# Layer 0's weight product on 64-row halves of the TensorE array, and the first hop tile by tile

## The chip, the cores and the metric

The kernel runs on one core of a Trainium2 chip. The metric is the device time of one execution in microseconds (us); lower is better. Times quoted as "median" are over several executions; the profile is of one execution, whose own time is given beside its span (the time from its first to its last instruction).

## The reference, cut to what matters

Two graph layers on x of shape (8, 2048, 64), with one adjacency matrix of 2048 x 2048, all in fp32. Each layer needs the features x, one hop A x and a second hop 2 A (A x) - x; it multiplies the three by weights, adds a bias and the input, and normalises each row of 64.

```python
# layer 0: the weights differ from node to node, through an embedding of D = 16
w   = einsum('nd,dkio->nkio', embedding, weight)      # K = 3 terms
b   = einsum('nd,do->no', embedding, bias)
x_g = stack of x, A x, 2 A (A x) - x
x   = layernorm(x + einsum('bnki,nkio->bno', x_g, w) + b)
# layer 1: one weight for all nodes; both supports are the same A, so five terms fold to three
x_cat = concat(x, Ax, 2AAx - x, Ax, 2AAx - x)
x   = layernorm(x + x_cat @ weight + bias)
```

## The kernel before, in words

The 2048 nodes are cut into 16 tiles `t` of 128 partitions. `z[t]` is a resident SBUF tile that holds for each of the 8 batches the 64 features of x (slot 0) and the 64 of A x (slot 1), interleaved: its shape is [128, 8, 2, 64]. A block of the adjacency is 128 columns of output by all 2048 rows, 1 MB, cut by `k` into 16 squares of 128 x 128.

`hop(t, s, ks)` (L122 to L129) sums 16 fp32 matmuls over `k` into one PSUM bank: stationary operand the square `blocks[t][:, k, :]`, moving operand the 512 columns of `z[k]`, slot `s`. The profile counts every fp32 matmul as two MATMUL records and two LDWEIGHTS records.

Each layer has two passes over the tiles. The first pass forms A x and copies it by ScalarE into slot 1 (L245). The second pass (L254 to L265) forms A A x; VectorE makes `x2` from it (L259). The weight product of a tile runs one tile behind: `transposes` (L131 to L144) turns `z[t]` and `x2` on TensorE, 12 transposes of 128 x 128 a tile, and ScalarE copies the results to SBUF as `t01` (for each batch 64 rows of x above 64 rows of A x) and `t2` (64 rows of an even batch above 64 of the odd one). Then `mix0` or `mix1` follows.

`mix0` (L180 to L199, layer 0) loops over 4 pairs of batches and 2 halves of D: 8 groups a tile. A group fills a PSUM tile `pm` of two banks, bank `j` for batch `j` of the pair: L189 does two matmuls with a contraction of 128 rows (x and A x together, against `w01`), L192 two with 64 rows (the second hop, against `w2`), the even batch on rows 0 to 63, the odd one on rows 64 to 127. VectorE then folds the group with 8 instructions (L196), one for each d, each multiplying 128 columns of `pm` by a column of the embedding and adding them to slot 0 of `z[t]` in place. The pool `ps_mix` holds two such groups. `layernorm` (L146 to L178) ends the tile with VectorE, GpSimd and ScalarE.

`mix1` (L201 to L219, layer 1) sums 12 matmuls a tile into one bank: 4 of 128 columns against `v2` (two copies of the weight on the diagonal) and 8 of 64 columns against `v01`.

[...]The first 8 blocks stay for the whole run in `low` (8 MB); the other 8 go through a pool of `SLOTS = 4` buffers, loaded again in every pass by `load_high` on SP's queue.

The start: 16 transfers of x on ScalarE's queue (L53, 256 KB each, in rows of 256 B because `z` is interleaved) and 16 on SP's queue (L54), each with square `k` of all 8 low blocks (512 KB in rows of 512 B). `first_sums` (L224 to L237) uses them as they come: for each `k`, 8 matmuls, one into each of the 8 PSUM banks (two of each of the three pools). The second half of the first hop, the 8 high tiles, follows tile by tile. The parameters (embedding, `w01`, `w2`, bias, `v01`, `v2`) come on GpSimd's queue.

The order of instructions on each engine is set by the tile scheduler at build time. On TensorE the order around the change is: `first_sums` with the bias matmuls (L96, L119) between them, eight hops, then for each tile transposes, hop and `mix0`.

Of the kernel before, what the change touches and what calls it, by code (L numbers as in the profile page):

```python
# [8 lines left out]
F32 = mybir.dt.float32  # L9
AF = mybir.ActivationFunctionType  # L10
ALU = mybir.AluOpType
# [3 lines left out]
P = 128  # L15
B, N, C = 8, 2048, 64
NT = N // P
D = 16
EPS = 1e-5
LOW = 8  # L20
SLOTS = 4
# [3 lines left out]
def gnn_kernel(  # L25
# [22 lines left out]
    z = [zpool.tile([P, B, 2, C], F32, tag=f"z{t}", name=f"z{t}") for t in range(NT)]  # L48


    low = zpool.tile([P, LOW, NT, P], F32, tag="low", name="low")
    for k in range(NT):
        nc.scalar.dma_start(out=z[k][:, :, 0, :], in_=x[k])  # L53
        nc.sync.dma_start(out=low[:, :, k, :], in_=adj[0:LOW, :, k, :].rearrange("t m n -> m t n"))  # L54
    apool = ctx.enter_context(tc.tile_pool(name="adj", bufs=SLOTS))
    blocks = {t: low[:, t] for t in range(LOW)}

    def load_block(t, tag):
        a = apool.tile([P, NT, P], F32, tag="a", name=f"a{t}_{tag}")
        nc.sync.dma_start(out=a, in_=adj[t])  # L60
        blocks[t] = a

    high = list(range(LOW, NT))

    def load_high(i, tag):
        if i < NT - LOW:
            load_block(high[i], tag)

    for i in range(SLOTS):
        load_high(i, 0)  # L70
# [6 lines left out]
    w01 = const.tile([P, D, C], F32, tag="w01", name="w01")  # L77
    w2 = const.tile([P, D, C], F32, tag="w2", name="w2")
    v01 = const.tile([P, C], F32, tag="v01", name="v01")
    v2 = const.tile([P, P], F32, tag="v2", name="v2")  # L80
    bias1 = const.tile([P, C], F32, tag="bias1", name="bias1")

    nc.gpsimd.dma_start(out=emb_sb, in_=emb.rearrange("(t p) d -> p t d", p=P))
    for k in range(2):
        nc.gpsimd.dma_start(out=w01[k * C : (k + 1) * C], in_=w0[:, k].rearrange("d i o -> i d o"))
    for h in range(2):
        nc.gpsimd.dma_start(out=w2[h * C : (h + 1) * C], in_=w0[:, 2].rearrange("d i o -> i d o"))
# [3 lines left out]
    for g in range(2):  # L91
        eT = work.tile([D, N // 2], F32, tag="t01", name=f"eT{g}")
        nc.gpsimd.dma_start(out=eT, in_=embT[:, g * (N // 2) : (g + 1) * (N // 2)])
        pb = ps_tp.tile([P, 8, C], F32, tag="tp", name=f"pb{g}")
        for j in range(8):
            nc.tensor.matmul(pb[:, j, :], lhsT=eT[:, j * P : (j + 1) * P], rhs=b0_sb, start=True, stop=True)  # L96
        nc.vector.tensor_copy(ebias[:, g * 8 : (g + 1) * 8, :], pb)


    v01b = work.tile([P, C], F32, tag="x2", name="v01b")  # L100
    nc.vector.memset(v01b, 0.0)
    nc.gpsimd.dma_start(out=v01, in_=w1[0 : 2 * C, :])
    nc.gpsimd.dma_start(out=v01b[C:P, :], in_=w1[3 * C : 4 * C, :])
    nc.vector.tensor_add(v01, v01, v01b)
    v2b = work.tile([P, P], F32, tag="t2", name="v2b")
    nc.vector.memset(v2, 0.0)
    nc.vector.memset(v2b, 0.0)
    for h in range(2):
        q = slice(h * C, (h + 1) * C)
        nc.gpsimd.dma_start(out=v2[q, q], in_=w1[2 * C : 3 * C, :])  # L110
        nc.gpsimd.dma_start(out=v2b[q, q], in_=w1[4 * C : 5 * C, :])
    nc.vector.tensor_add(v2, v2, v2b)
# [8 lines left out]

    def hop(t, s, ks):  # L122

        ph = ps_hop.tile([P, B, C], F32, tag="hop", name="ph")
        for j, k in enumerate(ks):
            nc.tensor.matmul(  # L126
                ph, lhsT=blocks[t][:, k, :], rhs=z[k][:, :, s, :], start=(j == 0), stop=(j == NT - 1)
            )
        return ph  # L129

    def transposes(t, x2):  # L131

        t01 = work.tile([P, B, P], F32, tag="t01", name="t01")
        t2 = work.tile([P, B // 2, P], F32, tag="t2", name="t2")
        for g in range(2):
            pt = ps_tp.tile([P, 4, P], F32, tag="tp", name="pt")
            for j in range(4):
                nc.tensor.transpose(pt[:, j, :], z[t][:, g * 4 + j, :, :], ident)  # L138
            nc.scalar.copy(t01[:, g * 4 : (g + 1) * 4, :], pt)  # L139
        pt = ps_tp.tile([P, 4, P], F32, tag="tp", name="pt")  # L140
        for j in range(4):
            nc.tensor.transpose(pt[:, j, :], x2[:, 2 * j : 2 * j + 2, :], ident)  # L142
        nc.scalar.copy(t2, pt)
        return t01, t2  # L144
# [35 lines left out]
    def mix0(t, t01, t2):  # L180

        acc = z[t][:, :, 0, :]
        nc.gpsimd.tensor_tensor(acc, acc, ebias[:, t : t + 1, :].to_broadcast([P, B, C]), ALU.add)  # L183
        for bp in range(B // 2):
            for dh in range(2):
                pm = ps_mix.tile([P, 2, D // 2, C], F32, tag="mix", name="pm")
                ds = slice(dh * (D // 2), (dh + 1) * (D // 2))
                for j in range(2):
                    nc.tensor.matmul(pm[:, j], lhsT=t01[:, 2 * bp + j, :], rhs=w01[:, ds, :], start=True, stop=False)  # L189
                for j in range(2):  # L190
                    q = slice(j * C, (j + 1) * C)
                    nc.tensor.matmul(pm[:, j], lhsT=t2[q, bp, :], rhs=w2[q, ds, :], start=False, stop=True)  # L192
                part = acc[:, 2 * bp : 2 * bp + 2, :]
                for d in range(D // 2):
                    dd = dh * (D // 2) + d
                    nc.vector.scalar_tensor_tensor(  # L196
                        part, pm[:, :, d, :], emb_sb[:, t, dd : dd + 1], part, ALU.mult, ALU.add
                    )
        layernorm(acc, acc)  # L199

    def mix1(t, t01, t2):  # L201

        pm = ps_mix.tile([P, B, C], F32, tag="mix", name="pm1")
        for bp in range(B // 2):
            nc.tensor.matmul(  # L205
                pm[:, 2 * bp : 2 * bp + 2, :], lhsT=t2[:, bp, :], rhs=v2, start=(bp == 0), stop=False,
                skip_group_check=True,
            )
            for j in range(2):
                b = 2 * bp + j  # L210
                nc.tensor.matmul(  # L211
                    pm[:, b, :], lhsT=t01[:, b, :], rhs=v01, start=False, stop=(b == B - 1), skip_group_check=True
                )
        acc = work.tile([P, B, C], F32, tag="acc", name="acc")
        nc.gpsimd.tensor_tensor(acc, z[t][:, :, 0, :], bias1.unsqueeze(1).to_broadcast([P, B, C]), ALU.add)
        nc.vector.tensor_tensor(acc, pm, acc, ALU.add)
        y = work.tile([P, B, C], F32, tag="y", name="y")
        layernorm(y, acc)
        nc.gpsimd.dma_start(out=out[t], in_=y)  # L219

    ks = list(range(NT))
    order = list(range(LOW)) + high

    def first_sums():  # L224

        accs = [ps_hop.tile([P, B, C], F32, tag="hop", name="ph") for _ in range(2)]
        accs += [ps_tp.tile([P, B, C], F32, tag="tp", name="pt") for _ in range(2)]
        for _ in range(2):
            pm = ps_mix.tile([P, 2, B, C], F32, tag="mix", name="pm")
            accs += [pm[:, 0], pm[:, 1]]  # L230
        for k in ks:
            for t in range(LOW):
                nc.tensor.matmul(  # L233
                    accs[t], lhsT=low[:, t, k, :], rhs=z[k][:, :, 0, :], start=(k == 0), stop=(k == NT - 1)
                )
        for t in range(LOW):
            nc.scalar.copy(z[t][:, :, 1, :], accs[t])  # L237

    for layer, mix in enumerate((mix0, mix1)):

        if layer == 0:
            first_sums()
        for t in order[LOW:] if layer == 0 else order:
            ph = hop(t, 0, ks)
            nc.scalar.copy(z[t][:, :, 1, :], ph)  # L245
            if t in high:
                load_high(high.index(t) + SLOTS, 2 * layer)
        ks = order


        behind = None
        for i in range(SLOTS):
            load_high(i, 2 * layer + 1)
        for t in order:  # L254
            if behind is not None:
                tr = transposes(*behind)
            ph = hop(t, 1, ks)
            x2 = work.tile([P, B, C], F32, tag="x2", name="x2")
            nc.vector.scalar_tensor_tensor(x2, ph, 2.0, z[t][:, :, 0, :], ALU.mult, ALU.subtract)  # L259
            if t in high:  # L260
                load_high(high.index(t) + SLOTS, 2 * layer + 1)
            if behind is not None:
                mix(behind[0], *tr)
            behind = (t, x2)
        mix(behind[0], *transposes(*behind))  # L265
        for i in range(SLOTS):
            if layer == 0:
                load_high(i, 2)
# [29 lines left out]
```

## Time and profile before

| | us |
|---|---|
| median of 3 executions (lowest, highest) | 1397.78 (1396.38, 1402.31) |
| the profiled execution's own time | 1397.78 |
| its span | 1395.2 |
| from the start to the end of `first_sums` | 129.0 |
| second half of the first hop, 8 tiles | 129.0 to 238.7 |
| layer 0's second pass with `mix0`, 16 tiles at 40.0 each, the last without a hop of its own | 238.7 to 880.8 |
| layer 1's first pass, 16 hops | 880.8 to 1100.5 |
| layer 1's second pass with `mix1`, 16 tiles at 17.68 each | 1100.5 to 1375.2 |
| the last tile's product and normalisation, and the last store | 1375.2 to 1395.2 |

The 2.6 us between the profiled execution's time and its span lie before the first and after the last instruction. The stages are read from the timeline: a stage ends where TensorE begins the next one's matmuls. The granted TensorE clock is 0.996 of full speed over the span.

### The profile page before, as it was taken

What the parts mean: (1) busy time and instruction counts of PE and PEld (TensorE: products, weight loads), DVE (VectorE), ACT (ScalarE), POOL (GpSimd) and SP (SyncE); (2) the same over time, 40 slices, a digit from 0 to 9 for tenths busy, and PEclk for the clock granted to TensorE, in tenths of its full rate; (3) what the DMA queues carried; (4) which work ended last, traced back from release to release, by engine and by line L of the source; (5) the groups of instructions that cost most, each with busy time, mean ns of one, the idle gap of its engine ahead of it and who ended that gap; (6) DMA issues with size and microseconds to landing.
All of it is one profiled execution on the core that took longest, in us unless ns stands there. A gap on an engine that the chain in (4) does not pass through costs nothing.

```text
span 1395.2 us, 10043 instructions
## 1 busy us (share of the span) xinstructions
PE 1357.0 (97%) x3874; PEld 601.4 (43%) x3874; DVE 476.2 (34%) x1369; ACT 99.5 (7%) x194; POOL 126.9 (9%) x133
## 2 busy tenths in 40 slices
PE   7999999999999999999999999999999999999996
PEld 3444444433333333333333333444444455555553
DVE  0000000266766666667666668300000012222222
ACT  0001000010000000000000000000000001111111
POOL 2000000011000000000000000000000012222222
PEclk9999999999999999999999999999999999999998
DMA  9900212000000000000000000000012100012100
GB/s 227 296 0 0 91 61 90 0 1 0 0 1 0 0 1 31 31 1 30 31 31 30 31 31 1 0 0 0 31 67 84 61 8 16 16 46 70 51 16 23
DMA packets 39903, 52.40 MB, mean 38 GB/s; under 512 B 17936, under 2 KB 34400, under 8 KB 35760
## 3 DMA queue, kind: packets, MB, share of 16 engines
q1 hardware_dynamic: 21248, 41.95, 9.4%
q10 hardware_dynamic: 16640, 4.20, 1.7%
q0 software_dynamic: 1968, 5.63, 1.3%
q8 instruction: 30, 0.49, 0.1%
q14 instruction: 17, 0.14, 0.0%
HBM read 47.57 MB, written 4.19 MB: 37 GB/s over the span
## 4 chain that ended last, share of the span: by engine, by line
PE 92%; DVE 4%; issue 1%; DMA 1%; POOL 0%; ACT 0%; ACTq 0%; POOLq 0%; DVEq 0%
PE ph L126 55%; PE pm L189 15%; PE pm L192 8%; DVE z L196 4%; PE pm L233 4%; PE pt L138 2%; PE ph L233 2%; PE pt L233 2%; PE pm L211 2%; PE pm L205 1%; DMA z<-in_x 1%; PE pt L142 1%; PE pb L96 0%; POOL xc L160 0%; DVE ln_s L156 0%
## 5 line engine op out<-in xcount | busy, mean ns | idle before, releaser
L126 PE MATMUL ph<-z,a 128*128 128x512 f32 x1024 | 445.1, 592 | 0.0
L196 DVE SCALAR_TENSOR_TENSOR z<-pm,emb_sb,z 128x128 f32<-128x128 f32 x1024 | 359.0, 351 | 74.0 <-PE pm L192 33.6
L126 PE MATMUL ph<-z,low 128*128 128x512 f32 x768 | 335.3, 592 | 0.0
L126 PEld LDWEIGHTS ph<-z,a 128*128 128x128 f32 x1024 | 192.1, 190 | 229.6 <-issue 229.6
L189 PE MATMUL pm<-w,t 128*128 128x512 f32 x512 | 249.5, 609 | 15.7 <-DVE z L196 6.3
L259 DVE SCALAR_TENSOR_TENSOR x<-ph,z 128x512 f32<-128x512 f32 x32 | 22.1, 692 | 687.7 <-PE ph L126 687.7
L126 PEld LDWEIGHTS ph<-z,low 128*128 128x128 f32 x768 | 143.5, 190 | 170.4 <-issue 170.4
L189 PEld LDWEIGHTS pm<-w,t 128*128 128x128 f32 x512 | 88.0, 189 | 172.9 <-PE pm L192 91.0
L192 PE MATMUL pm<-w,t 64*128 64x512 f32 x512 | 144.5, 641 | 0.0
L139 ACT COPY t<-pt 128x512 f32<-128x512 f32 x64 | 34.4, 589 | 736.9 <-PE pt L138 736.9
L183 POOL TENSOR_TENSOR z<-z,ebias 128x512 f32<-128x512 f32 x16 | 20.4, 1275 | 714.5 <-PE pt L138 714.5
L192 PEld LDWEIGHTS pm<-w,t 64*128 64x128 f32 x512 | 38.5, 184 | 97.1 <-issue 97.1
L233 PE MATMUL pm<-z,low 128*128 128x512 f32 x128 | 58.6, 600 | 0.0
L160 POOL TENSOR_TENSOR xc<-acc,ln_nm 128x512 f32<-128x512 f32 x16 | 16.5, 1033 | 409.7 <-DVE ln_nm L158 405.3
L233 PE MATMUL ph<-z,low 128*128 128x512 f32 x64 | 33.8, 653 | 9.8 <-DMA z<-in_x 9.8
L164 DVE TENSOR_REDUCE ln_ss<-sq 128x8 f32<-128x512 f32 x32 | 21.9, 686 | 60.4 <-ACT sq L162 60.4
L233 PEld LDWEIGHTS pm<-z,low 128*128 128x128 f32 x128 | 25.0, 196 | 31.7 <-issue 31.6
L245 ACT COPY z<-ph 128x512 f32<-128x512 f32 x24 | 14.1, 586 | 307.0 <-PE ph L126 307.0
L211 PE MATMUL pm<-v,t 128*128 128x64 f32 x256 | 35.6, 262 | 0.0
L138 PE MATMUL pt<-ident,z 128*128 128x128 f32 x256 | 34.1, 276 | 0.0
L138 PEld LDWEIGHTS pt<-ident,z 128*128 128x128 f32 x256 | 28.4, 144 | 12.4 <-issue 12.4
L211 PEld LDWEIGHTS pm<-v,t 128*128 128x128 f32 x256 | 33.7, 192 | 0.0
(58 smaller groups left out, 363.1 us busy)
## 6 DMA issues: line engine op xcount, KB each, us to landing
a<-in_adj SPq DMA_DIRECT2D x32, 1024.0 KB, 4.8
low<-in_adj SPq DMA_DIRECT2D x16, 512.0 KB, 12.5
z<-in_x ACTq DMA_DIRECT2D x16, 256.0 KB, 12.9
out<-y POOLq DMA_DIRECT2D x16, 256.0 KB, 2.3
w<-in_w POOLq DMA_DIRECT2D x4, 256.0 KB, 10.1
emb_sb<-in_emb POOLq DMA_DIRECT2D x1, 128.0 KB, 9.3
eT<-in_embT POOLq DMA_DIRECT2D x2, 64.0 KB, 10.8
v<-in_w POOLq DMA_DIRECT2D x1, 32.0 KB, 8.0
```

Source lines behind the costliest of these rows:

```text
L126: nc.tensor.matmul(ph, lhsT=blocks[t][:, k, :], rhs=z[k][:, :, s, :], start=(j == 0), stop=(j == NT - 1))
L138: nc.tensor.transpose(pt[:, j, :], z[t][:, g * 4 + j, :, :], ident)
L139: nc.scalar.copy(t01[:, g * 4 : (g + 1) * 4, :], pt)
L160: nc.gpsimd.tensor_tensor(xc, src, wide(nm), ALU.add)
L164: nc.vector.tensor_reduce(ss, sq, AX.X, ALU.add)
L183: nc.gpsimd.tensor_tensor(acc, acc, ebias[:, t : t + 1, :].to_broadcast([P, B, C]), ALU.add)
L189: nc.tensor.matmul(pm[:, j], lhsT=t01[:, 2 * bp + j, :], rhs=w01[:, ds, :], start=True, stop=False)
L192: nc.tensor.matmul(pm[:, j], lhsT=t2[q, bp, :], rhs=w2[q, ds, :], start=False, stop=True)
L196: nc.vector.scalar_tensor_tensor(part, pm[:, :, d, :], emb_sb[:, t, dd : dd + 1], part, ALU.mult, ALU.add)
L211: nc.tensor.matmul(pm[:, b, :], lhsT=t01[:, b, :], rhs=v01, start=False, stop=(b == B - 1), skip_group_check=True)
L233: nc.tensor.matmul(accs[t], lhsT=low[:, t, k, :], rhs=z[k][:, :, 0, :], start=(k == 0), stop=(k == NT - 1))
L259: nc.vector.scalar_tensor_tensor(x2, ph, 2.0, z[t][:, :, 0, :], ALU.mult, ALU.subtract)
```

## The change

Layer 0's product is done wholly with a contraction of 64 rows. `z[t]` is now [128, 2, 8, 64], so that slot 0 and slot 1 are each 512 contiguous columns; a transpose of 128 columns takes one slot of two neighbouring batches, and all three terms come out as `t2` did: even batch above, odd batch below. A group of `mix0` is then 6 matmuls of 64 rows, alternating between the lower and the upper rows, against weights that are held twice, in both halves of the partitions (`w[0]`, `w[1]`, `w[2]`). `mix1` becomes 12 matmuls of 128 columns against block-diagonal weights `v[0]` to `v[2]`.

`first_sums` and `low` are gone. All 16 blocks go through one pool of 11 buffers; each pass begins with the 11 blocks that are still resident from the pass before (`next_order`), and loads 5. The first pass is 16 plain hops. SP's queue begins with 11 transfers of 1 MB in rows of 8 KB; x comes on ScalarE's queue as before, now in rows of 2 KB. GpSimd's queue brings six transfers of 256 KB for layer 0's weights in place of four. On TensorE the built order now begins with tile 0's 16 matmuls, `k` from 0 to 15, then tile 1's, among which the bias matmuls come.

```diff
-LOW = 8
-SLOTS = 4
+SLOTS = 11
...
-    z = [zpool.tile([P, B, 2, C], F32, tag=f"z{t}", name=f"z{t}") for t in range(NT)]
-    low = zpool.tile([P, LOW, NT, P], F32, tag="low", name="low")
-    for k in range(NT):
-        nc.scalar.dma_start(out=z[k][:, :, 0, :], in_=x[k])
-        nc.sync.dma_start(out=low[:, :, k, :], in_=adj[0:LOW, :, k, :].rearrange("t m n -> m t n"))
...
+    z = [zpool.tile([P, 2, B, C], F32, tag=f"z{t}", name=f"z{t}") for t in range(NT)]
...
+    for t in range(NT):
+        nc.scalar.dma_start(out=z[t][:, 0], in_=x[t])
...
+    for k in range(3):
+        for h in range(2):
+            nc.gpsimd.dma_start(out=w[k][h * C : (h + 1) * C], in_=w0[:, k].rearrange("d i o -> i d o"))
...
+    order = list(range(NT))
+    for i in range(SLOTS):
+        load_block(order[i], 0)
+
+    def next_order(o):
+        return o[NT - SLOTS :] + o[: NT - SLOTS]
...
+    def prefetch(o, i, tag):
+        if i + SLOTS < NT:
+            load_block(o[i + SLOTS], tag)
...
     def transposes(t, x2):
+        out = []
+        for s in range(3):
+            tt = work.tile([P, B // 2, P], F32, tag=f"t{s}", name=f"t{s}")
+            pt = ps_tp.tile([P, B // 2, P], F32, tag="tp", name="pt")
+            for j in range(B // 2):
+                pair = x2[:, 2 * j : 2 * j + 2, :] if s == 2 else z[t][:, s, 2 * j : 2 * j + 2]
+                nc.tensor.transpose(pt[:, j, :], pair, ident)
+            nc.scalar.copy(tt, pt)
+            out.append(tt)
+        return out
...
     (mix0)
-                for j in range(2):
-                    nc.tensor.matmul(pm[:, j], lhsT=t01[:, 2 * bp + j, :], rhs=w01[:, ds, :], start=True, stop=False)
-                for j in range(2):
-                    q = slice(j * C, (j + 1) * C)
-                    nc.tensor.matmul(pm[:, j], lhsT=t2[q, bp, :], rhs=w2[q, ds, :], start=False, stop=True)
+                for k in range(3):
+                    for j in range(2):
+                        q = slice(j * C, (j + 1) * C)
+                        nc.tensor.matmul(
+                            pm[:, j], lhsT=tt[k][q, bp, :], rhs=w[k][q, ds, :], start=(k == 0), stop=(k == 2)
+                        )
...
     (mix1)
+            for k in range(3):
                 nc.tensor.matmul(
+                    pm[:, 2 * bp : 2 * bp + 2, :], lhsT=tt[k][:, bp, :], rhs=v[k],
+                    start=(bp == 0 and k == 0), stop=(bp == B // 2 - 1 and k == 2), skip_group_check=True,
                 )
...
-    def first_sums():
-        accs = [ps_hop.tile([P, B, C], F32, tag="hop", name="ph") for _ in range(2)]
-        accs += [ps_tp.tile([P, B, C], F32, tag="tp", name="pt") for _ in range(2)]
-        for _ in range(2):
-            pm = ps_mix.tile([P, 2, B, C], F32, tag="mix", name="pm")
-            accs += [pm[:, 0], pm[:, 1]]
-        for k in ks:
-            for t in range(LOW):
-                nc.tensor.matmul(
-                    accs[t], lhsT=low[:, t, k, :], rhs=z[k][:, :, 0, :], start=(k == 0), stop=(k == NT - 1)
-                )
-        for t in range(LOW):
-            nc.scalar.copy(z[t][:, :, 1, :], accs[t])
...
+        for i, t in enumerate(order):
             ph = hop(t, 0, ks)
+            nc.scalar.copy(z[t][:, 1], ph)
+            prefetch(order, i, 2 * layer)
         ks = order
+        order = next_order(order)
```

## The prediction

> **What bounds the kernel now.** I read the page first, then the timeline of one tile of layer 0, then the start and its transfers.
>
> ```profile
> PE 1357.0 (97%) x3874; PEld 601.4 (43%) x3874; DVE 476.2 (34%) x1369; ACT 99.5 (7%) x194; POOL 126.9 (9%) x133
> L196 DVE SCALAR_TENSOR_TENSOR z<-pm,emb_sb,z 128x128 f32<-128x128 f32 x1024 | 359.0, 351 | 74.0 <-PE pm L192 33.6
> L189 PE MATMUL pm<-w,t 128*128 128x512 f32 x512 | 249.5, 609 | 15.7 <-DVE z L196 6.3
> ```
>
> TensorE looks like the bound everywhere, at 97%. That is an average. Only L189 shows it waiting for VectorE, and that is the stage that the change rewrites. The timeline of one tile there (start, length, both in us):
>
> ```profile
> 267.50 1.88 PE L189 MATMUL pm<-w,t 128*128 128x512 f32 x4
> 269.31 1.13 PE L192 MATMUL pm<-w,t 64*128 64x512 f32 x4
> 270.37 1.98 PE L189 MATMUL pm<-w,t 128*128 128x512 f32 x4
> 270.60 21.84 DVE L196 SCALAR_TENSOR_TENSOR z<-pm,emb_sb,z 128x128 f32<-128x128 f32 x56 [2.21 <-PE pm L192]
> 272.29 1.13 PE L192 MATMUL pm<-w,t 64*128 64x512 f32 x4
> 273.80 1.96 PE L189 MATMUL pm<-w,t 128*128 128x512 f32 x4 [0.39 <-DVE z L196]
> 276.96 1.95 PE L189 MATMUL pm<-w,t 128*128 128x512 f32 x4
> ...
> 289.54 1.96 PE L189 MATMUL pm<-w,t 128*128 128x512 f32 x4 [0.19 <-DVE z L196]
> 291.42 1.13 PE L192 MATMUL pm<-w,t 64*128 64x512 f32 x4
> 292.48 1.09 PE L138 MATMUL pt<-ident,z 128*128 128x128 f32 x8
> ```
>
> VectorE folds 56 slices in 21.84 us, 0.390 each from start to start, so a group of 8 takes it 3.12. From 273.80 to 289.54 TensorE begins a group every 3.15 (15.74 / 5): VectorE's pace. TensorE itself needs less: the second group's L189 begins at 270.37, 2.87 after the first, and a group that follows another takes 289.54 to 292.48 = 2.94. Inside it one record costs 0.43 (a hop of 32 takes 13.73). L192's four records take only 1.06 (269.31 to 270.37), two slots of 0.43 and 0.2 more: lower and upper half do run side by side. So the product is bound by VectorE by 0.2 us a group, and by TensorE only at its two ends.
>
> The start is bound by transfers. The first two lines give issue length in ns (least/median/most) and the first and last issue in us; the next two give count, KB each and median us to landing; the last two are windows whose final figure is GB/s.
>
> ```profile
> L53 ACTq DMA_DIRECT2D z<-in_x x16: 635/2926/6362, 0.7 to 49.5; - x16
> L54 SPq DMA_DIRECT2D low<-in_adj x16: 424/2837/7294, 0.7 to 47.9; - x16
> low<-in_adj SPq DMA_DIRECT2D x16, 512.0 KB, 12.5
> z<-in_x ACTq DMA_DIRECT2D x16, 256.0 KB, 12.9
> 48.00:50.00 2.00, 2.00 (x6) 0.87 (x5) 0.00 (x0) 0.00 (x0) 0.00 (x0) 1.00 1.26 261
> 62.00:64.00 2.00, 2.00 (x6) 0.86 (x5) 0.00 (x0) 0.00 (x0) 0.00 (x0) 1.00 1.05 435
> ```
>
> The two queues advance together, although each transfer of x carries half the bytes of one of `low`. What is equal is the number of rows (1024 of 256 B against 1024 of 512 B). So the engines share by packets, not by bytes. TensorE nevertheless keeps busy from 17.5 on, because each x tile that lands feeds eight sums.
>
> **What the Trainium skill says.** "DMA: Bandwidth & Descriptors", section "Queues, rings and completion order": every DMA engine goes round the queues that have work, packet by packet. The trace agrees: 49.5 and 47.9 us for equal numbers of packets of unequal size. "TensorE: Matmul & The Clock Gate", section "Part 3: Packing small matmuls — row/col tiling": matmuls on different row groups run at once. The trace agrees for a burst of four (1.06 us); it has no longer run. "TensorEngine Tiling (Array Packing)", section "Key Properties": changing the tiling mode drains the array. The trace fits: four L189 records between two changes take 1.92 (270.37 to 272.29), not 1.72, so 0.1 at each side. "VectorE: DVE Perf Modes", section "Mode 1× (REGULAR) — the baseline": the plain mode makes no assumption on strides and takes PSUM operands as they are; the trace agrees that strides cost it nothing, since L259 with a strided operand and L216 without take 692 ns alike.
>
> **The change part by part.**
>
> *mix0 on TensorE.* Removed: 4 records of 128 rows a group (4 x 0.43 = 1.72) and 4 of 64 rows in pairs (2 x 0.43). Added: 12 records of 64 rows, in pairs 6 x 0.43 = 2.58. The slots are the same six; two terms stacked in 128 rows and two batches side by side in 64 rows are equal work. What goes is the mode changes, four times 0.1 a group, so 2.94 becomes about 2.58. Six of the eight groups wait for VectorE, which keeps 8 x 0.390. Its first fold starts when the first group is done, as before about 3.1 after the hop (0.1 change, 5 x 0.43, 0.70 for the last pair, 0.16 to the release: 3.11). The last group costs 2.78 with its exit change instead of 2.94. That is 0.16 a tile, 16 tiles: -2.5 us. Bounds: no pair gains anything beyond this because VectorE paces; if a load of weights showed in each slot (0.53, as in L192's first slot) a group would take 3.2 and pass VectorE: 8 x 3.2 + 0.3 - 24.98 = +0.9 a tile, +14. No overlap at all is a rival below.
>
> *The fold on VectorE.* 1024 instructions stay; the sum they add to is now contiguous. I take 351 ns unchanged, from L259 and L216 above. Bound below: the plain 159 + 128 / 0.96 = 292 that L216's 692 for 512 columns implies; rival below. Above: nothing is added.
>
> *The start.* What lands: x 4.2 MB in rows of 2 KB, 11 blocks 11.5 MB in rows of 8 KB, parameters 2.0 MB (six weights of 0.26, embedding and its transpose 0.26, the rest 0.2), 17.7 MB. Rows are few and long, so I take 410 GB/s from the windows from 60 to 68 us (406 to 435): 43.2 us, from 2.3 on. Packet by packet, x gets 2 KB for each 8 KB: it has 2048 packets against the blocks' 1408, so it ends last, after everything else: 45.5, and about 1 to its release. Tile 0 needs all sixteen x, and nothing in TensorE's queue can pass it: tile 1 and the bias matmuls stand behind. So TensorE idles: it has 16 matmuls where it had 128. Tile 0 ends at 47.4 (0.86 for the last matmul). Then 15 hops of 13.73 = 205.9, the bias matmuls 4.2 (before: 1.93 + 1.93 + 0.36, also exposed), and 1.6 because TensorE comes out of a sparse stretch at half clock (four records took 3.48 at 17.54, 1.88 later). First hop ends at 259.1; before at 238.7. +20.4. Bounds: at 435 GB/s -2.5; at the 350 of the whole window from 60 to 70, +7. Shared by bytes: rival.
>
> *Later loads.* 5 blocks a pass instead of 8, each issued on SP after a hop and needed eleven tiles on; landing takes 4.8 us, a hop 13.73. Hidden, before as well. If that cover went, a load would show at most 4.8. ScalarE issues 16 x transfers of 128 rows instead of 1024 and has nothing waiting behind them. GpSimd's two more weights delay the bias and `v` loads, needed after 47.
>
> *Transposes and copies.* 12 and 3 a tile as before; same sizes. Nil.
>
> *mix1.* 24 records a tile before and after. Four L211 of 64 columns and two L205 of 128 come every 0.67 (1127.92, 1128.59), so 0.11 a record, and 128 columns need 0.43 / 4 = 0.107. Nil; at the worst +0.1 a tile.
>
> *Sum.* +20.4 - 2.5 = +17.9 on a span of 1395.2, 1413.1; with the 2.6 around it 1415.7. The profiled execution's 1397.78 is also the median. What is late next after the start is TensorE's own row of hops, which has no slack to give back.
>
> **The rivals.**
> *A: x comes early.* If the queues shared bytes evenly, x would be in after twice 4.2 MB and 1 MB of parameters, 9.4 / 0.41 = 23 and 2.3: 25.3. Tile 0 ends near 27, and the time is 1415.7 - 20 = 1395.5, no change. It decides from x landing before some 27.6 us on. Against it: the two queues in step. For it: the sizes were 1 : 2, not 1 : 4.
> *B: weight loads show in every slot,* 0.53: 1397.8 + 20.4 + 14 = 1432. For it: L192's first slot. Against: L189's later records keep 0.43.
> *C: halves do not overlap in a long run:* a group 12 x 0.43 = 5.16, 41.3 a tile instead of 24.98, +261: 1680. Against it: L192's burst of two halves times two passes.
> *D: the contiguous fold is quicker,* 0.33 from start to start: six groups a tile gain 0.48, 16 tiles: -46, 1370. Against it: L259 shows no price of strides.
>
> **How the numbers follow.** Likeliest case 0.70, A 0.10, B 0.08, C 0.05, D 0.05, rest 0.02. The likeliest case's own bounds are 1410 to 1424. The range is 1400 to 1432: it holds that case, B and the cases between it and A. A measurement can tell about 0.5% here, 1390.8 to 1404.8. Faster: D and a little, 0.07. Same: A and part of the way to it, 0.14. Slower: 0.79.
>
> **What would show it.** Right: tile 0's sixteen matmuls spread over some 45 us with waits for x, first hop ending near 259; L188 groups 3.12 apart, TensorE waiting for VectorE, tiles of 39.8; layer 1 as before. Wrong: x landed by 27 us (A), groups of 3.2 (B) or 5.2 (C) without waits for VectorE, folds under 351 ns (D).

## The result, and the profile after

| | before | after |
|---|---|---|
| median of 4 executions each, us | 1400.05 (1396.38 to 1403.19) | 1416.81 (1413.22 to 1417.09) |
| the profiled execution's own time | 1397.78 | 1413.22 |
| its span | 1395.2 | 1411.4 |

The ratio is 1.0115 (95% interval 1.0081 to 1.0148): slower, by about what was forecast. The profiled execution is the quickest of the four. Its mean granted clock is 0.994; the other three have 0.990 and take 3.5 to 3.9 us more. No trace of after shows in which stage; the traces of its variants point to the end of layer 0 (below).

The two timelines, cut where TensorE begins the next stage, give the account in us. The first row ends one hop later than the prediction's "first hop ends".

| stage | before | after | difference |
|---|---|---|---|
| to the first transposes of layer 0's second pass | 252.46 | 271.98 | +19.52 |
| from there to layer 1's first matmul | 628.34 | 622.43 | -5.91 |
| from there to layer 1's first transposes | 231.85 | 232.71 | +0.86 |
| the rest | 282.57 | 284.32 | +1.75 |
| span | 1395.2 | 1411.4 | +16.2 |

The second and third rows do not compare like with like. Before starts one more matmul of layer 1's first hop inside layer 0's last tile:

```profile
860.40 1.13 PE L126 MATMUL ph<-z,low 128*128 128x512 f32 x2
```

Its two records stand for 0.86 us. Counted with layer 1 in both kernels, the second row is -5.05 and the third nothing.

The page of after, in the order of the lines shown of before (engines with busy time, share and instructions; then groups with busy time, mean ns of one, idle time ahead of them and its releaser):

```profile
PE 1342.0 (95%) x4386; PEld 629.0 (45%) x4386; DVE 473.6 (34%) x1373; ACT 99.7 (7%) x194; POOL 131.5 (9%) x141
L121 PE MATMUL ph<-z,a 128*128 128x512 f32 x2048 | 901.7, 598 | 22.2 <-DMA z<-in_x 22.2
L194 DVE SCALAR_TENSOR_TENSOR z<-pm,emb_sb,z 128x128 f32<-128x128 f32 x1024 | 354.6, 350 | 70.9 <-PE pm L188 32.5
L188 PE MATMUL pm<-w,t 64*128 64x512 f32 x1536 | 359.9, 602 | 33.4 <-DVE z L194 29.7
```

TensorE fell from 97% to 95%. The hop L121 now stands idle for 22.2 us, all of it for x. A fold still takes 350 ns. The product L188 waits 29.7 us for VectorE: halves of 64 rows have not made TensorE the bound of that stage.

The start of after (start and length in us; in brackets the idle time ahead and what ended it):

```profile
6.68 2.08 PE L121 MATMUL ph<-z,a 128*128 128x512 f32 x2 [6.68 <-DMA z<-in_x]
12.67 2.07 PE L121 MATMUL ph<-z,a 128*128 128x512 f32 x2 [3.91 <-DMA z<-in_x]
...
24.92 8.55 PE L121 MATMUL ph<-z,a 128*128 128x512 f32 x16 [4.14 <-DMA z<-in_x]
34.55 1.12 PE L121 MATMUL ph<-z,a 128*128 128x512 f32 x2 [1.07 <-DMA z<-in_x]
37.73 1.78 PE L121 MATMUL ph<-z,a 128*128 128x512 f32 x2 [2.05 <-DMA z<-in_x]
40.89 2.08 PE L121 MATMUL ph<-z,a 128*128 128x512 f32 x2 [1.39 <-DMA z<-in_x]
44.05 12.66 PE L121 MATMUL ph<-z,a 128*128 128x512 f32 x24 [1.08 <-DMA z<-in_x]
```

Tile 0's 32 records (two a matmul) are spread from 6.68 to about 46, each lot behind an x tile, as forecast; rival A, x in by 27 us, is out. The last line holds tile 0's last matmul and then tile 1, which starts at once. What moved the transfers (windows; the last three figures are granted clock, busy share of the DMA engines, GB/s):

```profile
2.00:10.00 8.00, 2.08 (x2) 0.50 (x2) 0.00 (x0) 0.00 (x0) 6.38 (x10) 1.00 0.99 326
10.00:20.00 10.00, 5.44 (x6) 1.50 (x6) 0.00 (x0) 0.00 (x0) 2.49 (x5) 1.00 1.05 241
20.00:30.00 10.00, 5.86 (x10) 2.28 (x10) 0.00 (x0) 0.91 (x1) 1.03 (x2) 1.00 1.04 324
30.00:40.00 10.00, 6.38 (x13) 1.81 (x11) 0.00 (x0) 0.37 (x1) 0.00 (x0) 0.90 1.01 412
40.00:46.00 6.00, 4.02 (x5) 1.42 (x6) 0.00 (x0) 0.00 (x0) 0.00 (x0) 0.50 1.02 419
```

The DMA engines are busy throughout, but from 10 to 20 us they move only 241 GB/s. That is where layer 0's weights, in rows of 256 B, are under way on GpSimd's queue; the last lands at 24.4 us. The queues from 10 to 20 us, and then from 34.5 to 44 us (packets, MB, share of the 16 engines' time; q0 is GpSimd's queue, q1 SP's with the blocks, q10 ScalarE's with x):

```profile
q0 software_dynamic: 387, 1.26, 55.4%
q10 hardware_dynamic: 392, 0.70, 31.6%
q1 hardware_dynamic: 70, 0.44, 18.3%
```

```profile
q1 hardware_dynamic: 440, 3.21, 81.7%
q10 hardware_dynamic: 410, 0.74, 20.8%
```

First 0.70 MB of x take 31.6% of 160 us of engine time, 50.6 us; later 0.74 MB take 20.8% of 152 us, 31.6 us. The blocks go from 67 to 39 us a MB. So GpSimd's queue does not only take its turns: while it runs, a row of the other queues takes 1.7 times as long.

By 45 us the windows add up to 14.5 MB, not the 17.7 of the prediction: the last four blocks land after x, at 45.7 to 53.1. SP's own waits in the first 75 us (total, times, longest) show why:

```profile
SPq L106 <- DMA z<-in_x: 36.5, 8, 13.3
```

SP has nothing to do with x, and still waits for its landings before it issues blocks: block 2 is issued at 12.6 and block 3 at 26.3, when x tiles land. I read that as completion semaphores which transfers of the two queues share.

One tile of layer 0 after, beside the one of before in the prediction:

```profile
287.12 5.42 PE L188 MATMUL pm<-w,t 64*128 64x512 f32 x24
290.08 24.56 DVE L194 SCALAR_TENSOR_TENSOR z<-pm,emb_sb,z 128x128 f32<-128x128 f32 x64 [2.17 <-PE pm L188]
293.28 2.85 PE L188 MATMUL pm<-w,t 64*128 64x512 f32 x12 [0.74 <-DVE z L194]
296.44 5.81 PE L188 MATMUL pm<-w,t 64*128 64x512 f32 x24 [0.31 <-DVE z L194]
302.56 5.80 PE L188 MATMUL pm<-w,t 64*128 64x512 f32 x24 [0.31 <-DVE z L194]
308.68 2.85 PE L188 MATMUL pm<-w,t 64*128 64x512 f32 x12 [0.31 <-DVE z L194]
```

Two groups of 12 records take 5.42 when nothing holds them up (2.7 each, forecast 2.58 to 2.78), so the halves run side by side; rival B, groups of 3.2, is out. From 293.28 to 308.68 a group begins every 3.08 (15.40 / 5); before it was 3.15. VectorE's 64 folds now form one unbroken row; before, it broke off ahead of the last eight.

Where the faster product gives some of its gain back, the end of layer 0:

```profile
876.25 2.85 PE L188 MATMUL pm<-w,t 64*128 64x512 f32 x12 [3.60 <-DVE z L194]
```

The built order now puts the whole layernorm of tile 14 on VectorE ahead of tile 15's folds; before, six folds of tile 15 lay within it. TensorE's row of tile 15 is held up for 3.60 us, where the same place in before had 0.63 and the early matmul of layer 1.

In this profile the clock stays at full speed there. In seven of the eight profiles below that have the changed product, all but the one on one half, it falls to half for 3.4 or 6.8 us around the end of this wait. In the last kernel built on after (x first, `w` late) the line is

```profile
854.61 7.12 PE L188 MATMUL pm<-w,t 64*128 64x512 f32 x24 [3.61 <-DVE z L194]
```

where 24 records elsewhere take 5.80. The second pass of these seven is 623.90 to 625.15, that of after 622.43. The longer time of after's other three executions would fit this; it isn't shown for them.

### The profile page after: what moved, and what is told of

The parts are those of the page before. It is cut to its first block, busy times and chain, and to the rows that moved or that the text cites. A ratio compares the mean times of both kernels' runs of the same rounds, so it can differ in the third digit from the quotient of the medians.

```text
span 1411.4 us, 11078 instructions
## 1 busy us (share of the span) xinstructions
PE 1342.0 (95%) x4386; PEld 629.0 (45%) x4386; DVE 473.6 (34%) x1373; ACT 99.7 (7%) x194; POOL 131.5 (9%) x141
## 5 line engine op out<-in xcount | busy, mean ns | idle before, releaser
L121 PE MATMUL ph<-z,a 128*128 128x512 f32 x2048 | 901.7, 598 | 22.2 <-DMA z<-in_x 22.2
L121 PEld LDWEIGHTS ph<-z,a 128*128 128x128 f32 x2048 | 385.6, 191 | 490.4 <-issue 455.4
L188 PE MATMUL pm<-w,t 64*128 64x512 f32 x1536 | 359.9, 602 | 33.4 <-DVE z L194 29.7
L188 PEld LDWEIGHTS pm<-w,t 64*128 64x128 f32 x1536 | 153.0, 186 | 238.6 <-issue 132.9
L139 ACT COPY t<-pt 128x512 f32<-128x512 f32 x96 | 52.9, 585 | 742.8 <-PE pt L138 742.1
L204 PE MATMUL pm<-v,t 128*128 128x128 f32 x384 | 45.7, 275 | 0.3 <-ACT t L139 0.3
L159 ACT ACTIVATE sq<-xc 128x512 f32<-128x512 f32 x32 | 20.2, 630 | 85.2 <-POOL xc L157 85.2
L157 POOL TENSOR_TENSOR xc<-z,ln_nm 128x512 f32<-128x512 f32 x16 | 16.7, 1041 | 58.2 <-DVE ln_nm L155 58.2
L210 DVE TENSOR_TENSOR acc<-pm,acc 128x512 f32<-128x512 f32 x16 | 11.1, 691 | 30.7 <-PE pm L204 30.7
L175 POOL TENSOR_TENSOR z<-xc,ln_r 128x512 f32<-128x512 f32 x16 | 16.7, 1042 | 49.8 <-DVE ln_r L174 49.8
L209 POOL TENSOR_TENSOR acc<-z,bias 128x512 f32<-128x512 f32 x16 | 20.4, 1273 | 1.3
```

The source lines that it names most:

```text
L121: nc.tensor.matmul(ph, lhsT=blocks[t][:, k, :], rhs=z[k][:, s], start=(j == 0), stop=(j == NT - 1))
L139: nc.scalar.copy(tt, pt)
L157: nc.gpsimd.tensor_tensor(xc, src, wide(nm), ALU.add)
L159: nc.scalar.activation(sq, xc, AF.Square)
L188: nc.tensor.matmul(pm[:, j], lhsT=tt[k][q, bp, :], rhs=w[k][q, ds, :], start=(k == 0), stop=(k == 2))
L204: nc.tensor.matmul(pm[:, 2 * bp : 2 * bp + 2, :], lhsT=tt[k][:, bp, :], rhs=v[k], start=(bp == 0 and k == 0), stop=(bp == B // 2 - 1 and k ...
```

## The experiments

My theory after the result: the loss is the start, and within it the order of packets in the DMA engines; the product gains a little more than forecast. Rivals: the loss is in the number of sums that each x tile feeds (`first_sums` is gone), or in the parameters. Ratios are against before, timed in the same rounds; after itself was timed only in the four executions above, so a difference of a few us to its median says little. "First pass" is the first transposes of the second pass (before 252.46, after 271.98), "tile" the period of layer 0's second pass (39.99 and 39.53).

**Do the halves run side by side in a long row?** Odd batches read the lower rows too, so the odd half of the product is left out and the even one done twice; for the rest it is after.

```diff
-                        q = slice(j * C, (j + 1) * C)
+                        q = slice(0, C)
```

> The changed kernel, but layer 0's product takes rows 0 to 63 for the odd batches too: they get the even batches' features and weights in the lower rows, so the odd half of the product is left out and the even one done twice; counts and shapes of all instructions stay. Theory (the two halves of the array run side by side, two records in 0.43 us): without the second half a group takes 12 x 0.43 = 5.2 in place of 2.6, a tile 41.3 + 15 = 56 in place of 39.5, time 1680. Rival (the halves do not overlap in a long run and the pace was VectorE's anyway): about 1417.

Measured in one execution: 1682.35 us, a tile of 56.59. Its timeline, one tile's product, first on TensorE and then one group of its folds on VectorE:

```profile
286.11 41.46 PE L188 MATMUL pm<-w,t 64*128 64x512 f32 x96
```

```profile
296.72 3.05 DVE L194 SCALAR_TENSOR_TENSOR z<-pm,emb_sb,z 128x128 f32<-128x128 f32 x8 [2.02 <-PE pm L188]
```

On one half, 96 records need 96 x 0.432 = 41.46, and VectorE stands 2 us ahead of each group of eight folds (3.05 of work in 5.15). With two halves the same records lie within 24.4 (287.12 to 311.53). So they do overlap over a whole tile, which before's burst of four had only suggested. Rival C is out.

**Is the gain of the product the mode changes alone?** Before, with the order of the 128-row and the 64-row matmuls turned round in every second group, so that half of the changes go.

```diff
+                for half in (0, 1) if dh == 0 else (1, 0):
+                    first = half == (0 if dh == 0 else 1)
...
-                    nc.tensor.matmul(pm[:, j], lhsT=t01[:, 2 * bp + j, :], rhs=w01[:, ds, :], start=True, stop=False)
+                            nc.tensor.matmul(pm[:, j], lhsT=t01[:, 2 * bp + j, :], rhs=w01[:, ds, :], start=first, stop=not first)
```

> The kernel before, but in every second group of the product the 64-row matmuls come first and the 128-row ones last, so that neighbouring groups meet in the same mode: about one change of tiling mode a group in place of two. Theory (the changed kernel's tile of 39.5 in place of 40.0 comes from TensorE's mode changes, whose 0.1 us each stand in the round trip between TensorE and VectorE): a tile of about 39.7, time 5 below the kernel before, 1395. Rival (it comes from the fold's contiguous operand): tiles stay at 40.0, time as before, 1400.

Measured: 1396.73, ratio 0.9988 (0.9976 to 0.9999), tile 39.91: 0.08 of the 0.3 that I expected. The folds, taken one by one from the trace, say why. Where the next batch pair begins, two of the three gaps between folds fell (403, 381 and 361 ns from start to start, in before 403, 401 and 398). At the other boundaries the last three rose (473, 496 and 562, in before 456, 458 and 512). From its first start to its last the row of 64 folds takes 24.75 us, against 24.70 before and 24.22 after.

The changes that this kernel takes out stand between groups, where TensorE waits for VectorE anyway. The change inside a group stays: from its first record to the start of its last a group takes 2.43 or 2.45 us here, 2.43 in before and 2.26 in after. So fewer changes between groups do not shorten VectorE's row; the change inside a group was not tested alone.

**Is the start lost to the order of the transfers?** After, with block 0 first and x next on both queues, ahead of all other blocks.

```diff
-    for i in range(SLOTS):
+    load_block(order[0], 0)
+    for t in range(NT):
+        (nc.scalar if t % 2 == 0 else nc.sync).dma_start(out=z[t][:, 0], in_=x[t])
+    for i in range(1, SLOTS):
         load_block(order[i], 0)
```

> The changed kernel, but SP's queue sends block 0, then the odd tiles of x, and only then blocks 1 to 10; ScalarE's queue sends the even tiles of x. Theory (x is late because the DMA engines alternate between queues packet by packet, and a block's row of 8 KB stands against each 2 KB of x): x, block 0 and the parameters are 7.2 MB, in by about 20 us, tile 0 ends near 23 instead of 46, and the time falls by 23 from the changed kernel's 1416.8, to 1394 (1390 to 1397). Rival (the start is lost because only one sum is open at a time in place of eight, whenever x comes): tile 0 still ends after 35, time above 1405.

Measured: 1408.04, ratio 1.0068 (1.0049 to 1.0088), first pass 262.74. Its timeline and its window from 10 to 20 us:

```profile
24.89 17.43 PE L121 MATMUL ph<-z,a 128*128 128x512 f32 x40 [1.68 <-DMA z<-in_x]
...
48.87 1.07 PE L73 MATMUL pb<-b_sb,eT 16*128 16x64 f32 x8 [1.85 <-DMA eT<-in_embT]
```

```profile
10.00:20.00 10.00, 8.14 (x9) 2.85 (x10) 0.00 (x0) 0.00 (x0) 2.38 (x5) 1.00 1.05 225
```

Only nine of the lost 19 us came back; tile 0 ended at 32.9, not 23. Although x stood ahead of all blocks but one, the window moved 225 GB/s with its engines busy: the parameters on GpSimd's queue take their share. Then the bias matmuls wait for the embedding at 48.87, which after did not.

**Does a packet count, or a byte?** After, with each first block loaded in four pieces, so that its rows are 2 KB like those of x.

```diff
-        nc.sync.dma_start(out=a, in_=adj[t])
+        n = NT // parts
+        for i in range(parts):
+            nc.sync.dma_start(out=a[:, i * n : (i + 1) * n, :], in_=adj[t][:, i * n : (i + 1) * n, :])
...
-        load_block(order[i], 0)
+        load_block(order[i], 0, 4)
```

> The changed kernel, but each of the first 11 blocks is sent as four transfers with rows of 2 KB in place of one with rows of 8 KB; order, queues and bytes stay. Theory (packets alternate): x now gets a third to a half of the bandwidth until it is in, 2 x 4.2 MB and 2.0 of parameters, near 28 us; tile 0 ends near 30, time 1401 (1397 to 1405). Rival (queues share bytes, or all 17.7 MB have to land before tile 0 can end): x lands as in the changed kernel, tile 0 ends at 46, time 1417.

Measured: 1412.59, ratio 1.01 (1.0071 to 1.0129), first pass 269.34, tile 0 done at 39.1. Its timeline, when only the two queues are left:

```profile
33.94 1.12 PE L123 MATMUL ph<-z,a 128*128 128x512 f32 x2 [0.32 <-DMA z<-in_x]
35.38 1.12 PE L123 MATMUL ph<-z,a 128*128 128x512 f32 x2 [0.32 <-DMA z<-in_x]
36.84 15.10 PE L123 MATMUL ph<-z,a 128*128 128x512 f32 x34 [0.33 <-DMA z<-in_x]
```

x tiles come every 1.45 us, 262 KB / 1.45 = 181 GB/s of 387 moved, 47%. In after (34.55, 37.73, 40.89, 44.05) they come every 3.17, 83 of 414 GB/s, 20%. Rows of 2 KB against 2 KB give half, 2 KB against 8 KB give a fifth: the two queues move equal numbers of rows, as the prediction read it from before. In all three kernels a transfer of x also has as many rows as the transfer beside it, so the shares alone don't tell turns by rows from turns by transfers. The packets of after do: from 34 to 43.5 us, 89% of the rows of x are followed within 4 ns by the start of a block's row, where chance would give 27%. In this run there is no such pattern (40% against 35%); the turns are longer, though the counts come out equal. Tile 0 gains 7 us by it, of which 2.6 is left at the end of the first pass: the bias matmuls now wait 1.70 for their operands, and some 6.8 us pass at half clock.

**Are the sums per x tile what is missing?** After, with tiles 0, 1 and 2 summed at once, in three PSUM banks.

```diff
+            for k in ks:
+                for i in range(done):
+                    nc.tensor.matmul(
+                        accs[i], lhsT=blocks[i][:, k, :], rhs=z[k][:, 0], start=(k == 0), stop=(k == NT - 1)
+                    )
```

> The changed kernel with all its transfers as they are, but tiles 0 to 2 of the first hop are summed at once, in three PSUM banks, square by square of k. Theory (the waits for x stay, but a landed x then feeds three matmuls in place of one): three tiles end near 53 in place of 46 for one and 73 for three; 18 to 20 less, 1397 to 1400. Rival (transfers alone set the start, open sums do not matter): no change, 1417.

Measured: 1412.61, ratio 1.0103 (1.0077 to 1.0129), first pass 268.70. Missed by 12.6 us. Its timeline:

```profile
13.67 6.15 PE L225 MATMUL ph<-z,a 128*128 128x512 f32 x8 [5.09 <-DMA z<-in_x]
26.19 3.78 PE L225 MATMUL pm<-z,a 128*128 128x512 f32 x4 [6.37 <-DMA a<-in_adj]
```

x was no longer what was late; block 2 was. SP was held behind x for 37.5 us in all, so the block landed at 26.2, and TensorE stood until then. Three sums need three blocks early. The experiment doesn't say what three sums would gain with the blocks there.

**Is it the parameters?** After, with the six transfers of `w` (1.6 MB) on SP's queue behind the blocks.

```diff
-    for k in range(3):
-        for h in range(2):
-            nc.gpsimd.dma_start(out=w[k][h * C : (h + 1) * C], in_=w0[:, k].rearrange("d i o -> i d o"))
...
     for i in range(SLOTS):
         load_block(order[i], 0)
+    for k in range(3):
+        for h in range(2):
+            nc.sync.dma_start(out=w[k][h * C : (h + 1) * C], in_=w0[:, k].rearrange("d i o -> i d o"))
```

> The changed kernel, but layer 0's six weight transfers leave GpSimd's queue and stand on SP's behind the first 11 blocks. Theory (until about 24 us the parameters' rows of 256 B hold the DMA engines at 225 to 260 GB/s in the changed kernel, so x would come sooner without them): x then shares 410 GB/s with the blocks only, at one part in five while both queues are full; x is in by 38 to 41 us in place of 45 and the bias matmuls move into tile 0's waits; time 4 to 8 below the changed kernel, 1409 to 1413. Rival (the parameters cost nothing, only the order of blocks and x counts): 1417.

Measured: 1397.77, ratio 1.0 (0.9986 to 1.0014), first pass 255.70. Far more than expected: 16.3 of the 19.5 us of the first pass came back. Its window from 10 to 20 us:

```profile
10.00:20.00 10.00, 8.00 (x26) 4.37 (x27) 0.85 (x2) 0.00 (x0) 1.41 (x3) 1.00 1.06 375
```

375 GB/s where after had 241; x is in by 29 us and tile 0 ends at 36. SP still waits 22.4 us for x. The block rows are the same as in after, so most of the loss was not theirs alone: it hung on the weights, which GpSimd's queue brought in ahead of x although only the second pass needs them. Their short rows are not the whole of it. On SP's queue, from 48 to 54 us, the same rows of 256 B leave a block's row of 8 KB at 309 ns, by the packets of the trace; in after, beside GpSimd's queue, the median of such rows went up to 598. No run has the weights in long rows on GpSimd's queue. How much of the gain is rows that are no longer slowed, and how much SP's blocks being asked for at other times, this run doesn't separate.

**Both together.** After, with x first, `w` late, and the four pieces of the embedding's transpose in buffers of which none has to be waited for.

```diff
-        eT = work.tile([D, N // 4], F32, tag="acc", name=f"eT{g}")
+        eT = work.tile([D, N // 4], F32, tag="acc" if g < 2 else "t0", name=f"eT{g}")
```

> Both orders at once: x on both queues behind block 0 and ahead of the other blocks, layer 0's weights behind all blocks; the four pieces of the transposed embedding have a buffer each, so that none waits for a bias matmul. Theory (the start is bound by what stands in the queues ahead of the last x): 5.7 MB at 400 GB/s, x in by 17, tile 0 ends near 20 in place of 33 with x first alone and 46 in the changed kernel; first hop ends near 227, time 1386 to 1391, below both kernels. Rival (tile 0 cannot end before about 33 because TensorE runs at half clock while it waits): 1403 to 1408.

Measured: 1392.71, ratio 0.9964 (0.9952 to 0.9976), first pass 250.26; faster than before and after. Its timeline:

```profile
9.73 6.72 PE L121 MATMUL ph<-z,a 128*128 128x512 f32 x8 [1.10 <-DMA z<-in_x]
...
26.99 33.31 PE L121 MATMUL ph<-z,a 128*128 128x512 f32 x77
```

Tile 0 ends at 30.7, and from 9.73 on TensorE has no gap: with x in early, tile 1 and the bias matmuls follow at once. It missed the expectation by 2 us: x was in at 20.2 us and not 17, and TensorE runs at half clock until about 16 and for 3.4 us more at the end of layer 0. The first pass without `first_sums` is now shorter than before's with it (252.46), so the loss did not lie in the number of sums that an x tile feeds.

**The product without the new start, and before with the weights late.** Three kernels: before with the changed product but its own start (`first_sums`, `low`; `SLOTS = 3`, as the new weights need room); the same with `w` late; and before with nothing changed but its weights late, the last two with an edit of this kind:

```diff
-        nc.gpsimd.dma_start(out=w01[k * C : (k + 1) * C], in_=w0[:, k].rearrange("d i o -> i d o"))
+        nc.sync.dma_start(out=w01[k * C : (k + 1) * C], in_=w0[:, k].rearrange("d i o -> i d o"))
```

> The kernel before with the changed product alone: contiguous slots in z, all three terms on 64-row halves, block-diagonal weights in layer 1; the first sums in eight banks and the 8 resident blocks stay (3 buffers for the other blocks in place of 4, for room). Theory (the change is two parts that add up, +19.5 at the start and -0.49 a tile): tiles of 39.5, so -7 in layer 0, about +3 at the end of layer 0 and in layer 1 as in the changed kernel, and up to -5 at the start because x comes in rows of 2 KB in place of 256 B: 1391 to 1396. Rival (the product gains nothing by itself): 1400.

> The kernel before with the changed product alone, and layer 0's weights behind SP's first loads. Theory (what made the product alone 5 slower than the kernel before was its start, 8.8 later because 1.6 MB of weights and the longer rows of x went ahead of the resident blocks): the first hop now ends at 235 or before, and the 0.46 a tile saved in layer 0 remains; time 1385 to 1391, below all others. Rival (the longer rows of x alone hold back the 512 B rows of the resident blocks): start unchanged, 1400 to 1403.

> The kernel before, with its four transfers of layer 0's weights moved from GpSimd's queue to the end of SP's first loads. Theory (in both kernels the weights' rows of 256 B hold up x in the first 25 us): the waits for x of 13 us in the kernel before shrink to about 5, the first hop ends 6 to 9 earlier, time 1388 to 1392. Rival (only the changed kernel, with its single open sum, is hurt by them): as before, 1397.

| | time | ratio (95%) | first pass | tile |
|---|---|---|---|---|
| product alone | 1403.2 | 1.003 (1.0019 to 1.0042) | 261.24 | 39.53 |
| product alone, `w` late | 1396.11 | 0.9985 (0.997 to 1.0) | 251.55 | 39.54 |
| before, weights late | 1394.39 | 0.9962 (0.9949 to 0.9976) | 249.87 | 40.00 |

The tile of 39.53 ties the product's gain to the product and not to the start. But the product alone came out slower than before, because its start took 8.8 us more. The line that shows it is the first of k = 1 in the product alone:

```profile
21.14 3.75 PE L224 MATMUL ph<-z,low 128*128 128x512 f32 x4 [7.20 <-DMA low<-in_adj]
```

In before the same records began at 17.54 and waited for x; with before's weights late they begin at 13.77 without a wait. With x in rows of 2 KB and two more weight transfers it is the rows of `low` (512 B) that come late. The two queues of the product alone from 26 to 37 us, SP's first:

```profile
q1 hardware_dynamic: 3531, 1.78, 62.1%
q10 hardware_dynamic: 1015, 1.84, 48.9%
```

Here rows of 512 B and of 2 KB got equal bytes, four rows for one, so equal numbers of rows are no general rule. With the weights out of the way 9.7 us come back; before itself gains 2.6 by the same edit. On SP's queue the weights then come last, and with nothing else under way their rows of 256 B move at 187 GB/s with the engines busy (product alone, `w` late):

```profile
55.20:61.50 6.30, 6.30 (x16) 2.73 (x15) 0.00 (x0) 0.00 (x0) 0.00 (x0) 1.00 1.15 187
```

All three stayed above what I expected, by 7, 5 and 2 us. For the first I had taken before's start as given. The second's first hop ended at 237.8 us and not by 235. For the last I had counted on 6 to 9 us in the first hop, and it was 2.6.

Before with its weights late and after with x first and `w` late both beat before, and their intervals overlap. In the profiles they stand at spans of 1392.7 and 1391.4: the first pass is alike (249.87 and 250.26), and the second has the product's gain in the latter, 624.19 against 628.49. Of these 4.3 us, 0.86 is the matmul of layer 1 that before starts early, and the end of layer 1 takes 1.8 back (284.27 against 282.44), about as in after.

## Why the prediction was right, and where it was not

*The product, -2.5.* Six slots of 0.43 a group, equal work and halves that overlap: right (5.42 for two groups; 41.46 a tile without the overlap). VectorE paces: right; 3.08 a group, 0.31 us of wait ahead of most. The size was wrong: the tile went from 39.99 to 39.53, -0.46 where the prediction had -0.16, and the stage lost 5.91, like for like 5.05, in place of 2.5. The step that failed is "bound by VectorE by 0.2 us a group, and by TensorE only at its two ends". Within a group folds follow every 386 ns in both kernels, each adding to what the one before wrote. At the boundary in the middle of a batch pair it is 455 ns in both. At the boundary to the next pair, where the sum is another one, it was 398 to 403 ns in before and is 268 in after: VectorE could start such a fold before the last one was through, but in before TensorE's group was not ready. The signals in the trace show it: in before, the first fold of six of a tile's eight groups starts 25 ns after TensorE's release, just as in the run on one half, where TensorE is far behind; in after none does. So TensorE was also the later one at three places inside each tile: 3 x 0.13 and 0.06 at the last boundary (511 to 455) make 0.45. It adds up: two groups should take 14 x 0.386 + 0.455 + 0.268 = 6.13, and 296.44 to 302.56 is 6.12. A mean of 0.390 over 56 folds had hidden three gaps of one kind among others.

The prediction compared what each engine needs for a group, 2.94 and 3.12, and left out the hand-overs. With two buffers, the group after next waits for the folds of this one: 0.146 us from the end of a group's last fold to TensorE's next group in that buffer, 2.425 to the start of that group's last record, 0.638 to the first fold, 3.053 for eight folds. That is 6.26 for two groups, and 6.26 is the pace of before (14 x 0.386 + 0.455 + 0.401). With 2.257 in place of 2.425 the round trip of after would be about 6.09, an estimate with before's hand-overs, and VectorE's own 6.13 sets the pace. At layer 0's end about 1.9 us of the gain are given back (15 x 0.464 less 5.05).

*The fold unchanged:* right, 350 ns against 351. Rival D is out.

*The start, +20.4:* measured +19.5, and the stage that the prediction named ends at about 258.3 (271.98 less a hop), forecast 259.1. The mechanism is right in its core: tile 0 waits for all of x, x gets one row for each row of a block (a fifth of the bytes, and half when the blocks' rows were as short), and nothing in TensorE's queue passes it. But two terms of the sum were wrong and cancelled. The rate was not 410 GB/s from the start on: it was 338 on average to 46 us, because the rows of x and of the blocks are slowed while GpSimd's queue brings the weights (241 GB/s). And x was not last of all: SP's issue was held behind x landings, so the last blocks came later, and x needed 14.5 MB to pass instead of 17.7. 14.5 / 0.338 = 43, the forecast 17.7 / 0.41 = 43 again. That the two cancel is luck. With the weights out of the way 16.3 us of it go, so the parameters deserved a step of their own: the prediction counted their bytes and not what their queue does to the others. The same omission has a part in my misses with x first and with the product alone.

*Bias matmuls and half clock, 4.2 and 1.6:* right together. From tile 0's end at 46.1 to 258.3 are 212.2, less 15 hops of 13.73 leaves 6.3. The windows show half clock from about 38 to 48. The Trainium skill, "TensorE: Matmul & The Clock Gate", section "What's actually happening", has the clock at half after an idle window of some 3.4 us; the trace goes further, since gaps of 1 to 2 us between pairs of records went with half clock (the pair at 40.89 takes 2.08, the one at 34.55 took 1.12). At the end of layer 0 a wait of 3.6 us went with half clock in seven profiles and not in after's.

*Later loads, transposes, ScalarE:* nil, as forecast. *Layer 1:* nil was forecast. The +0.86 is the matmul that before starts early; the hops themselves are unchanged. Of the +1.75 after them 0.7 lies in the tiles (17.73 against 17.68, within the +0.1 a tile that was allowed for) and 1.05 behind them: the last tile's add on VectorE (L210) stands behind the whole layernorm of the tile before it. The built order did that, not the cost of a matmul.

*The sum* was 1413.1 for the span and came to 1411.4: 0.9 less at the start and, like for like, 2.6 less in the product than forecast, 1.75 more at the end of layer 1.

## What to carry to other kernels

When a start is bound by transfers, look at rows and queues before bytes: here a queue of transfers that weren't needed yet slowed those that were, and moving them behind the others brought back 16.3 of 19.5 us. When two engines alternate, look at the gaps at each kind of boundary one by one; a mean over a row of instructions does not tell which engine was late at which of them, and with a fixed number of buffers the round trip with its hand-overs can be slower than either engine. A change that saves on one engine can be lost in a start or an order that it moves along with it, so it is worth building each part alone.

## What the runs showed of the hardware

- A transfer on SP's queue waited for landings of transfers on ScalarE's queue (36.5 us in after), although no data passed between them.
- While GpSimd's queue brought the weights in rows of 256 B, the DMA engines were busy and moved 225 to 241 GB/s (10 to 20 us in after and x first); without the weights, 375; with SP's and ScalarE's queues alone, 412 to 419. A row of the other queues took 1.7 times as long meanwhile (after). Rows of 256 B alone on SP's queue moved 187 GB/s.
- The Trainium skill's page "DMA: Bandwidth & Descriptors", section "SWDGE vs HWDGE vs iDMA", gives a packet, the unit at which an engine turns to another queue, as preferably at most 4096 B and at most 64 descriptors. By that figure two rows of 2 KB would make a packet, and x would have had a third of the bytes beside rows of 8 KB (an estimate); it had a fifth, one row for one. Rows of 2 KB beside rows of 512 B had half of the bytes (the product alone). What rule covers both was not settled.
- The granted clock of the windows stands at 1.00 up to 30 us in after, though the pairs at 6.68 to 18.70 took 2.08, the length of those at half clock; the trace's first record of the clock is at 27.8. The length of a record tells the clock there, not the view of it.
- In after, a fold whose sum the fold before has just written begins 386 ns after it; one with an independent sum, 268 ns, less than its own 350 ns.
